# A four-layer graph attention stack: how feature blocks are turned in the third and fourth layer

## The chip, the cores and the metric

The kernel runs on one core of one Trainium2 chip. The metric is the device time of one launch in microseconds (us), from the runs listed below. The engines are named as the profile names them: PE (TensorE, the matrix unit), DVE (VectorE), ACT (ScalarE), POOL (GpSimd) and SP (SyncE). DMAs are issued by an engine, here by SP or POOL, and carried out by 16 DMA engines. Each engine works off its own list of instructions in order; between engines there are semaphores.

## The reference

`x` has 4096 rows (the nodes) of 256 features in float32; `adj` is a 4096 x 4096 matrix of 0 and 1. Four attention layers follow each other, each over all pairs of nodes that `adj` joins, and each ends with a residual sum and a layer norm. The change touches the third and the fourth layer:

```python
# third layer: one additive head
h = x @ W
e = leaky_relu(h @ a[:D, 0] [:, None] + h @ a[D:, 0] [None, :], slope 0.01)
x = layernorm(x + elu(softmax(where(adj > 0, e, -1e12), axis=1) @ h))

# fourth layer: cosine attention
Qn, Kn = cos_normalize(x @ Wq.T), cos_normalize(x @ Wk.T)     # 128 features each
att = softmax(where(adj > 0, Kn @ Qn.T, -9e15), axis=1)
x = layernorm(x + 0.5 * (att @ x) + 0.5 * x)
```

The first layer is additive with four heads, the second is multi-head attention with four heads of 64.

## The kernel before

The features stay in SBUF as `X`, 32 tiles of 128 rows (NT = 32). Four tiles make a block of 512 rows (QB = 4), so there are eight blocks (NB = 8). A projection by PE contracts over features, so it needs a block with the features on the partitions: the block has to be *turned* (transposed) before it. There are two ways to do this in the kernel.

- `transposed_block` (L112): PE transposes eight 128 x 128 pieces into PSUM (L118), and DVE and ACT copy one half each into SBUF (L120). This gives `xT`.
- `turned_apart` (L123), called by `block_apart` (L138) for a block of `X`: DVE transposes 32 x 32 squares within the tiles (two instructions, L130) into a buffer `squares`, one DMA writes it to DRAM (`squares_far`, L133), and four DMAs bring it back, 32 partitions each (L135). The 512 rows of the block come back in another order: the row `k*128 + a*32 + n` of the block stands in tile `a` at place `k*32 + n` (`k` and `a` from 0 to 3, `n` from 0 to 31). A sum over the rows does not depend on their order, so the result is the same if masks, `src`, `dst` and values all keep to it.

**Third layer, `additive_one` (L401).** The loop goes over blocks `b` of columns and, inside, over 32 tiles `j` of rows: 256 units. For each unit ACT forms `e` from the row vector `row` and the scalar `dst` (L451), DVE adds 1 and multiplies by the mask, giving `prob` (L453), and PE adds `prob` times the values `V` into four PSUM accumulators (`sums`, L459, four matmuls). `prob` has three buffers (`gb_z`). A mask tile holds two units, 128 x 2 x 512 int32 or 512 KB, and SP loads it (L449) into one of four buffers. The values `V`, `src` and `dst` of a block come from `project` (L427, matmuls at L196, then ACT at L200 to L202 and DVE at L203). `fill_row` (L431) spreads `src` over all partitions: for block 0 and 1 by PE (L441), for the later ones by two DMAs on POOL's queue, `far<-src` (L436, 512 elements of 4 bytes to DRAM) and `row<-far` (L437, back to 128 partitions).

Blocks 0 and 1 are turned and projected before the loop. Block `n` (2 to 7) is prepared inside `b = 0`: `turn(n)` at `j = 4(n - 2)`, `project(n)` and `fill_row(n)` at `j = 4(n - 2) + 2`. At `j` = 0, 3 and 5 of `b = 0`, the last block of the second layer is finished (`tail`): two sums on POOL (L687), the second of which waits for a DMA, then row sums and turned halves on PE.

**Fourth layer.** Its preparation is class `Cosine`. `prepare(bank, b, step)` (L837) has three steps for each block: step 0 turns the block of `X` (`block_apart`), step 1 projects it (L852), squares and sums it (L857), copies it (L858), takes the roots and multiplies (L863), step 2 turns the result into `T` (`turned_apart`). For blocks 0 to 5 the steps stand in the last block of the third layer (`b = 7`, and step 0 of the first ones at the end of `b = 6`): step 1 of block `n` after unit `2 + 4n`, step 2 after unit `5 + 4n`, step 0 eight units before step 1. Blocks 6 and 7 are prepared in `cosine_attention`, in its first block. All turnings share one `squares` buffer (`co_once`, one buffer). Blocks 0 to 5 issue their DMAs on POOL's queue, blocks 6 and 7 on SP's.

The order of PE's instructions is written by hand in the third layer (`manual_schedule` for PE); for the other engines a scheduler decides it, by what is ready.

Of the kernel before, what the change touches and what calls it, by code (L numbers as in the profile page):

```python
# [9 lines left out]
FP = mybir.dt.float32  # L10
# [8 lines left out]
P = 128  # L19
D = 256  # L20
KC = D // P
QB = 4
QW = QB * P
# [5 lines left out]
def kernel(  # L29
# [27 lines left out]
    nc = tc.nc  # L57
    N = x.shape[0]
    NT = N // P
    NB = N // QW  # L60

    def pool(stack, name, bufs, **kw):
        return stack.enter_context(tc.tile_pool(name=name, bufs=bufs, reuse_waits="tile", **kw))
# [48 lines left out]
    def transposed_block(sb, bank, b, copies=(nc.vector.tensor_copy, nc.scalar.copy)):  # L112

        xT = sb.tile([P, KC * QW], FP, name="xT").rearrange("p (c i) -> p c i", c=KC)
        pts = [bank() for _ in range(KC)]
        for c, pt in enumerate(pts):
            for k in range(QB):
                nc.tensor.transpose(pt[:, k * P:(k + 1) * P], X[:, b * QB + k, c * P:(c + 1) * P], ident)  # L118
        for c, pt in enumerate(pts):
            copies[c](xT[:, c, :], pt)  # L120
        return xT.rearrange("p c (k i) -> p c k i", i=P)

    def turned_apart(once, dr, part, to, eng):  # L123

        B = P // QB
        squares = once.tile([P, QB, KC, P], FP, name="squares")
        for c in range(KC):
            nc.vector.transpose(squares[:, :, c, :].rearrange("p q (k n) -> p k q n", n=B),  # L130
                                part(c).rearrange("p k (q f) -> p k q f", f=B))
        far = dr.tile([QB, B, QB, KC * P], FP, name="squares_far")
        eng.dma_start(far.rearrange("a f q m -> (a f) (q m)"), squares.rearrange("p q c m -> p (q c m)"))  # L133
        for q in range(QB):
            eng.dma_start(to[q * B:(q + 1) * B], far[:, :, q, :].rearrange("a f m -> f a m"))  # L135
        return to.rearrange("p a (c m) -> p c a m", c=KC)
# [264 lines left out]
    def additive_one(w_sb, slope, tail, op, follow):  # L401

        MJ = 2
        mvs, taken = {}, {}
        with ExitStack() as lay:
            keep = pool(lay, "gb_keep", 1)
            V = keep.tile([P, NT, D + 1], FP, name="V")
            src = keep.tile([P, NT, 1], FP, name="src")
            dst = keep.tile([P, NT, 1], FP, name="dst")
            row = keep.tile([P, N], FP, name="row")  # L410
            zp = pool(lay, "gb_z", 3)
            sb = pool(lay, "gb_sb", 2)
            mp = pool(lay, "gb_mask", 4)
            dr = pool(lay, "gb_dram", 2, space=bass.MemoryType.DRAM)

            ps = pool(lay, "gb_ps", 4, space=PSUM)
            pa = pool(lay, "gb_pa", 1, space=PSUM)
            edges = adjT.rearrange("(t p) i -> p t i", p=P)
            mask, acc, prob = {}, {}, {}

# [1 line left out]
                return ps.tile([P, QW], FP, name="g")  # L422

            def turn(b):
                return transposed_block(sb, bank, b)

            def project(b, xT, ks=range(QB)):  # L427
                groups = [(k, 1, bank().rearrange("p (n f) -> p n f", n=1)) for k in ks]
                additive_values(xT, b, groups, w_sb, V, src, dst, 1, slope)

            def fill_row(b):  # L431
                part = row[:, b * QW:(b + 1) * QW]
                if b > 1:

                    far = dr.tile([QB, P], FP, name="far")
                    nc.gpsimd.dma_start(far.rearrange("k p -> p k"), src[:, b * QB:(b + 1) * QB, 0])  # L436
                    nc.gpsimd.dma_start(part, far.rearrange("k p -> (k p)").unsqueeze(0).to_broadcast([P, QW]))  # L437
                    return
                pr = bank()
                for k in range(QB):  # L440
                    nc.tensor.transpose(pr[:, k * P:(k + 1) * P], src[:, b * QB + k, :].to_broadcast([P, P]), ident)  # L441
                nc.scalar.copy(part, pr)

            def weights(b, j):
                cols = slice(b * QW, (b + 1) * QW)
                m = b, j // MJ
                if j % MJ == 0:
                    mask[m] = mp.tile([P, MJ, QW], I32, name="mask")
                    nc.sync.dma_start(mask[m], edges[:, j:j + MJ, cols])  # L449
                e = sb.tile([P, QW], FP, name="e")  # L450
                nc.scalar.activation(e, row[:, cols], AF.Relu, bias=-1.0, scale=dst[:, j, :])  # L451
                prob[b, j] = zp.tile([P, QW], FP, name="prob")
                nc.vector.scalar_tensor_tensor(prob[b, j], e, 1.0, mask[m][:, j % MJ, :], OP.add, OP.mult)  # L453
# [27 lines left out]
            units = [(b, j) for b in range(NB) for j in range(NT)]  # L481
            with tc.manual_schedule(engines={mybir.EngineType.PE}):
                xTs = {0: turn(0), 1: turn(1)}
                project(0, xTs[0])
                project(1, xTs[1], [0, 1])
                fill_row(0)
                project(1, xTs[1], [2, 3])
                for i in range(len(units) + 1):
                    if i < len(units):
                        b, j = units[i]  # L490
                        weights(b, j)

                        if b == 0 and j // QB + 2 < NB:
                            n = j // QB + 2
                            if j % QB == 0:
                                xTs[n] = turn(n)
                            elif j % QB == 2:
                                project(n, xTs[n])
                                fill_row(n)
                    if i:  # L500
                        b, j = units[i - 1]
                        sums(b, j)
                        if (b, j) == (0, 1):
                            fill_row(1)
                        if b == 0 and j in (0, 3, 5):
                            tail(bank, (0, 3, 5).index(j))
                            if j == 5:
                                follow.start()
                        if b and j % 4 == 0 and j // 4 < QB:
                            outputs(b - 1, j // 4)  # L510
                        n, rest = divmod(i - (NB - 1) * NT + 5, 4)
                        if rest == 0 and 0 <= n < NB - 2:
                            follow.prepare(even_bank, n, 0)
                        if b == NB - 1:
                            if j in (6, 10, 14):
                                follow.load_mask(0, (j - 6) // 4, prob[b, j][:, :1])


                            for step, first in enumerate((2, 5), 1):
                                if j >= first and (j - first) % 4 == 0 and (j - first) // 4 < NB - 2:  # L520
                                    follow.prepare(even_bank, (j - first) // 4, step)
                        if j == NT - 1:
                            take_all(b)
# [285 lines left out]
    class Cosine:  # L809

        MJ = 4
# [5 lines left out]
        def start(self):  # L817
            keep = self.stack.enter_context(tc.tile_pool(name="co_keep", bufs=1, side="right", reuse_waits="tile"))
            self.pool = self.stack.enter_context(tc.tile_pool(name="co_in", bufs=2, side="right", reuse_waits="tile"))
            self.masks = self.stack.enter_context(tc.tile_pool(name="co_mask", bufs=4, side="right", reuse_waits="tile"))  # L820
            self.mask = {}

            self.T = [keep.tile([P, QB, 2 * P], FP, name=f"T{b}") for b in range(NB)]
            self.dram = self.stack.enter_context(tc.tile_pool(name="co_dram", bufs=2, space=bass.MemoryType.DRAM))
            self.once = self.stack.enter_context(tc.tile_pool(name="co_once", bufs=1, side="right", reuse_waits="tile"))
            self.w_sb = keep.tile([P, KC, 2 * P], FP, name="w3_sb")
            load_w(self.w_sb[:, :, :P], wq3T, nc.sync)
            load_w(self.w_sb[:, :, P:], wk3T, nc.sync)
# [8 lines left out]
        def prepare(self, bank, b, step):  # L837

            in_, w_sb = self.pool, self.w_sb

            eng = nc.gpsimd if b < NB - 2 else nc.sync
            if step == 0:
                self.xT[b] = block_apart(in_, self.once, self.dram, b, eng)
            elif step == 1:
                xT = self.xT.pop(b)
                norm = in_.tile([P, QB, 2], FP, name="norm")
                rows = self.rows[b] = in_.tile([P, QB, 2, P], FP, name="rows")
                for k in range(0, QB, 2):
                    pr = bank().rearrange("p (t n f) -> p t n f", t=2, f=P)
                    for t in range(2):  # L850
# [12 lines left out]
                nc.vector.tensor_tensor(flat, flat, r.unsqueeze(2).to_broadcast([P, QB * 2, P]), OP.mult)  # L863
            else:
                rows = self.rows.pop(b)
                turned_apart(self.once, self.dram, lambda n: rows[:, :, n, :], self.T[b], eng)

    def cosine_attention(co, tail):
        MJ = co.MJ
        T = [t.rearrange("p k (n i) -> p n k i", n=2) for t in co.T]  # L870
        with ExitStack() as lay:
            sb = pool(lay, "co_sb", 3)
            yp = pool(lay, "co_y", 2)

            pa = pool(lay, "co_pa", 1, space=PSUM)
            pz = pool(lay, "co_pz", 2, space=PSUM)
# [150 lines left out]
```

## Time and profile before

| what | us |
|---|---|
| median of three runs | 2911.56 |
| lowest and highest of them | 2909.53, 2911.84 |
| the profiled execution | 2912.43 |
| its span, first to last instruction | 2910.7 |

The profile is of one execution. A line of its groups names the code line, engine, operation and tile, then how often it ran, its busy time and the mean of one, and what ended the idle time before it. Mean durations of the groups concerned, in the third layer's stretch of the trace:

| group | mean us of one |
|---|---|
| L451, ACT, `e` | 0.721 |
| L453, DVE, `prob` | 0.695 |
| L459, PE, one matmul of 128 x 257 | 0.380 to be busy, 1.735 for the four of a unit and their weights |
| L130, DVE, stream transpose 128 x 512 | 0.69 |
| L120, DVE or ACT copy | 0.68, 0.58 |
| L133, POOL issue of `squares_far<-squares` | 0.56 |
| L135, POOL issue of one of four | 0.555 |
| L436, POOL issue of `far<-src` | 0.776 |

The mean granted clock of PE over the span is 0.997 of full speed.

### The profile page before, as it was taken

The page shows a single profiled execution, that of the slowest core. Times are in us where ns is not written, and L with a number is a line of the kernel's source. Part 1 is how long each engine was busy: PE and PEld are TensorE (multiplying, and loading weights), DVE is VectorE, ACT ScalarE, POOL GpSimd, SP SyncE. Part 2 cuts the span into 40 slices and gives each one's busy share as a digit, 9 for nine tenths or more (in the row PEclk, how much of TensorE's full clock was granted, in tenths as well). Part 3 has the DMA queues.
Part 4 walks back from the last instruction along what each step waited for, and adds up shares of the span by engine and source line. Part 5 has one row for each costly group of instructions (what it writes and reads, how often), then busy time and mean ns, then how long its engine had stood idle before and what let it go on. Part 6 is the DMA issues. An engine that isn't in the chain of part 4 may idle for free.

```text
span 2910.7 us, 50256 instructions
## 1 busy us (share of the span) xinstructions
PE 2889.4 (99%) x20141; PEld 1553.4 (53%) x20141; DVE 1954.2 (67%) x2541; ACT 1655.3 (57%) x2589; POOL 965.2 (33%) x735
## 2 busy tenths in 40 slices
PE   9999999999999999999999999999998999999998
PEld 4333333333643333333333358888887777777776
DVE  8899999998677777777777765655666423333333
ACT  7899999997356666666666654444443222222222
POOL 0010010100068989989889860000012000000000
PEclk9999999999999999999999999999999999999999
DMA  7566667665068989889889875655566434434341
GB/s 205 103 138 137 139 139 145 135 129 90 1 134 193 185 186 193 183 187 192 182 189 191 182 171 133 178 163 150 154 185 168 87 58 58 58 58 58 58 58 29
DMA packets 214061, 391.72 MB, mean 135 GB/s; under 512 B 16338, under 2 KB 94146, under 8 KB 212931
## 3 DMA queue, kind: packets, MB, share of 16 engines
q0 software_dynamic: 106336, 190.35, 40.2%
q1 hardware_dynamic: 107216, 197.88, 22.3%
q8 instruction: 158, 2.59, 0.3%
q14 instruction: 77, 0.62, 0.1%
q10 hardware_dynamic: 274, 0.26, 0.0%
HBM read 325.46 MB, written 29.43 MB: 122 GB/s over the span
## 4 chain that ended last, share of the span: by engine, by line
PE 98%; DMA 1%; DVE 1%; ACT 0%; issue 0%; POOL 0%; DVEq 0%; POOLq 0%
PE acc L293 23%; PE acc L901 15%; PE acc L678 15%; PE p L645 15%; PE acc L459 8%; PE g L459 7%; PE p L889 4%; PE g L889 3%; PE g L572 2%; PE g L196 1%; PE pv L587 1%; PE acc L196 1%; PE g L118 1%; PE acc L852 1%; DMA squares_far<-squares 1%; PE g L305 0%
## 5 line engine op out<-in xcount | busy, mean ns | idle before, releaser
L657 DVE TENSOR_TENSOR prob<-p,mask 128x1024 f32<-128x1024 f32 x512 | 624.1, 1223 | 209.5 <-ACT p L647 203.8
L647 ACT ACTIVATE p<-p,shift 128x1024 f32<-128x1024 f32 x512 | 556.2, 1088 | 325.2 <-PE p L645 324.4
L293 PE MATMUL acc<-prob,V 128*32 128x512 f32 x6144 | 664.0, 592 | 1.2 <-DVE prob L283 1.2
L664 POOL TENSOR_TENSOR den<-den,prob 128x1024 f32<-128x1024 f32 x248 | 626.9, 2528 | 72.6 <-DVE prob L657 64.7
L280 ACT ACTIVATE prob<-row,dst 128x512 f32<-128x512 f32 x1020 | 633.1, 712 | 0.1
L283 DVE SCALAR_TENSOR_TENSOR prob<-prob,mask 128x2048 f32<-128x2048 f32 x256 | 582.5, 2286 | 24.2 <-ACT prob L280 20.7
L645 PE MATMUL p<-qT,kT 64*64 64x512 f32 x4096 | 532.3, 590 | 0.8 <-DVE prob L657 0.8
L678 PE MATMUL acc<-prob,V 64*64 64x512 f32 x4096 | 531.5, 589 | 0.0
L901 PE MATMUL acc<-X,prob 128*128 128x257 f32 x2048 | 485.5, 380 | 0.0
L901 PEld LDWEIGHTS acc<-X,prob 128*128 128x128 f32 x2048 | 388.6, 190 | 162.8 <-issue 112.9
L894 DVE TENSOR_TENSOR prob<-prob,mask 128x512 f32<-128x512 f32 x256 | 176.2, 690 | 409.3 <-ACT prob L893 408.1
L293 PEld LDWEIGHTS acc<-prob,V 128*32 128x32 f32 x6144 | 197.3, 110 | 453.1 <-issue 433.6
L451 ACT ACTIVATE e<-row,dst 128x512 f32<-128x512 f32 x256 | 184.0, 721 | 241.8 <-DVE prob L453 212.6
L678 PEld LDWEIGHTS acc<-prob,V 64*64 64x64 f32 x4096 | 155.9, 133 | 285.4 <-issue 278.1
L645 PEld LDWEIGHTS p<-qT,kT 64*64 64x64 f32 x4096 | 154.4, 133 | 277.3 <-issue 261.5
L453 DVE SCALAR_TENSOR_TENSOR prob<-e,mask 128x512 f32<-128x512 f32 x256 | 177.6, 695 | 173.4 <-PE acc L459 93.9
L91 POOL COPY tick<-prob 128x1 f32<-128x1 f32 x35 | 40.0, 1144 | 645.9 <-DVE prob L283 644.8
L835 POOL DMA_DIRECT2D mask<-in_adjT x64 | 47.6, 743 | 582.2 <-DVE prob L894 505.3
L670 POOL DMA_DIRECT2D den<-prob x240 | 231.6, 965 | 14.7 <-DVE prob L657 7.5
L893 ACT ACTIVATE prob<-p 128x512 f32<-128x512 f32 x144 | 85.7, 596 | 257.0 <-PE p L889 243.0
L459 PE MATMUL acc<-V,prob 128*128 128x257 f32 x1024 | 225.1, 380 | 0.0
L459 PE MATMUL g<-V,prob 128*128 128x257 f32 x1024 | 224.1, 380 | 0.0
(160 smaller groups left out, 1965.6 us busy)
## 6 DMA issues: line engine op xcount, KB each, us to landing
mask<-in_adjT SPq DMA_DIRECT2D x256, 512.0 KB
den<-prob POOLq DMA_DIRECT2D x240, 512.0 KB, 5.3
mask<-edges SPq DMA_DIRECT2D x256, 128.0 KB
mask<-in_adjT POOLq DMA_DIRECT2D x64, 512.0 KB, 5.7
edges<-in_adj POOLq DMA_DIRECT2D x32, 512.0 KB, 10.0
den<-prob SPq DMA_DIRECT2D x16, 512.0 KB
row<-far SPq DMA_DIRECT2D x7, 1024.0 KB
squares_far<-squares POOLq DMA_DIRECT2D x12, 512.0 KB, 4.0
```

Source lines behind the costliest of these rows:

```text
L280: nc.scalar.activation(z[:, h, :], r, AF.Relu, bias=-1.0, scale=dst[:, j, h:h + 1])
L283: nc.vector.scalar_tensor_tensor(z, z, 1.0, mask[m][:, j % MJ, :].unsqueeze(1).to_broadcast([P, H, QW]), OP.add, OP.mult)
L293: nc.tensor.matmul(acc[b][h * G:(h + 1) * G, n, :], part, prob[b, j][:, h, :], start=(j == 0), stop=(j == NT - 1))
L459: nc.tensor.matmul(acc[b][k][:, :D + 1], prob[b, j][:, k * P:(k + 1) * P], V[:, j, :], start=(j == 0), stop=(j == NT - 1))
L645: nc.tensor.matmul(p[c * d:(c + 1) * d, r, :], kT[half, c, j * d:(j + 1) * d], qT[half, c, cols], start=True, stop=True)
L647: nc.scalar.activation(p, p, AF.Exp, bias=shift)
L657: nc.vector.tensor_tensor(z, p, mask[m][:, j % MJ, :].unsqueeze(1).to_broadcast([P, KC, QW]), OP.mult)
L664: nc.gpsimd.tensor_tensor(to, to, flat, OP.add)
L670: nc.gpsimd.dma_start(to, flat, accum_op=OP.add)
L678: nc.tensor.matmul(acc[b][c][r * d:(r + 1) * d, :], V[half, j, r * d:(r + 1) * d], prob[b, j][half, r, :], start=(j == 0), stop=(j == NH - 1))
L889: nc.tensor.matmul(p.rearrange("p (k i) -> p k i", k=QB), T[j // QB][:, 0, j % QB], T[b][:, 1], start=True, stop=True)
L901: nc.tensor.matmul(acc[b][k], prob[b, j][:, k * P:(k + 1) * P], X[:, j, :], start=(j == 0), stop=(j == NT - 1))
```

## The change

Three things are changed. Line numbers here are those of the kernel before.

1. Third layer: blocks 2 to 7 are turned by `block_apart` (DVE and POOL's queue) and not by PE. Block 2 is turned before the loop, block `n + 1` at `j = 4(n - 2)`, one group of four units ahead of its projection. The turning gets pools of its own: three `xT` buffers, one `squares` buffer, two DRAM buffers.
2. The rows of these blocks stand in the other order. Masks of rows from the ninth tile on are fetched by four DMAs of 32 partitions each, in the order of the turned block, and `far<-src` becomes four DMAs of 32 x 4 elements.
3. Fourth layer: step 0 is issued on SP's queue and uses the third layer's turning pools (later a set of the same in the fourth layer). Step 2 stays on POOL's queue (SP for blocks 6 and 7), with a squares buffer of its own. The tile `rows` comes from `co_once`, with one buffer and not two.

```diff
-    def turned_apart(once, dr, part, to, eng):
+    def turned_apart(squares, far, part, to, eng):
         B = P // QB
-        squares = once.tile([P, QB, KC, P], FP, name="squares")
+        squares = squares.tile([P, QB, KC, P], FP, name="squares")
+        far = far.tile([QB, B, QB, KC * P], FP, name="far")
...
+            xp = pool(lay, "gb_turn", 3)
+            sq = pool(lay, "gb_squares", 1)
+            far = pool(lay, "gb_far", 2, space=bass.MemoryType.DRAM)
+            follow.turning = xp, sq, far
...
+            apart = adjT.rearrange("(b k a n) i -> k n b a i", k=QB, a=QB, n=P // QB)
...
             def turn(b):
-                return transposed_block(sb, bank, b)
+                return transposed_block(xp, bank, b)
+            def turn_apart(b):
+                return block_apart(*follow.turning, b, nc.gpsimd)
...
-                    far = dr.tile([QB, P], FP, name="far")
-                    nc.gpsimd.dma_start(far.rearrange("k p -> p k"), src[:, b * QB:(b + 1) * QB, 0])
-                    nc.gpsimd.dma_start(part, far.rearrange("k p -> (k p)").unsqueeze(0).to_broadcast([P, QW]))
+                    far = dr.tile([QB, QB, P // QB], FP, name="far")
+                    for k in range(QB):
+                        at = slice(k * P // QB, (k + 1) * P // QB)
+                        nc.gpsimd.dma_start(far[k].rearrange("a n -> n a"), src[at, b * QB:(b + 1) * QB, 0])
+                    nc.gpsimd.dma_start(part, far.rearrange("k a n -> (k a n)").unsqueeze(0).to_broadcast([P, QW]))
...
                     mask[m] = mp.tile([P, MJ, QW], I32, name="mask")
-                    nc.sync.dma_start(mask[m], edges[:, j:j + MJ, cols])
+                    if j < 2 * QB:
+                        nc.sync.dma_start(mask[m], edges[:, j:j + MJ, cols])
+                    else:
+                        for k in range(QB):
+                            nc.sync.dma_start(mask[m][k * P // QB:(k + 1) * P // QB],
+                                              apart[k, :, j // QB, j % QB:j % QB + MJ, cols])
...
                 xTs = {0: turn(0), 1: turn(1)}
+                xTs[2] = turn_apart(2)
                 project(0, xTs[0])
...
                             n = j // QB + 2
-                            if j % QB == 0:
-                                xTs[n] = turn(n)
+                            if j % QB == 0 and n + 1 < NB:
+                                xTs[n + 1] = turn_apart(n + 1)
                             elif j % QB == 2:
                                 project(n, xTs[n])
                                 fill_row(n)
...
-            self.dram = self.stack.enter_context(tc.tile_pool(name="co_dram", bufs=2, space=bass.MemoryType.DRAM))
             self.once = self.stack.enter_context(tc.tile_pool(name="co_once", bufs=1, side="right", reuse_waits="tile"))
+            self.far = self.stack.enter_context(tc.tile_pool(name="co_far", bufs=2, space=bass.MemoryType.DRAM))
...
-            eng = nc.gpsimd if b < NB - 2 else nc.sync
             if step == 0:
-                self.xT[b] = block_apart(in_, self.once, self.dram, b, eng)
+                self.xT[b] = block_apart(*self.turning, b, nc.sync)
             elif step == 1:
...
-                rows = self.rows[b] = in_.tile([P, QB, 2, P], FP, name="rows")
+                rows = self.rows[b] = self.once.tile([P, QB, 2, P], FP, name="rows")
...
-                turned_apart(self.once, self.dram, lambda n: rows[:, :, n, :], self.T[b], eng)
+                turned_apart(self.once, self.far, lambda n: rows[:, :, n, :], self.T[b],
+                             nc.gpsimd if b < NB - 2 else nc.sync)
...
+            co.turning = (pool(lay, "co_turn", 2), pool(lay, "co_squares", 1),
+                          pool(lay, "co_turn_far", 2, space=bass.MemoryType.DRAM))
```

More of the change, by code (lines that the diff above doesn't have):

```diff
@@ L131, in turned_apart @@
                                 part(c).rearrange("p k (q f) -> p k q f", f=B))
-        far = dr.tile([QB, B, QB, KC * P], FP, name="squares_far")
         eng.dma_start(far.rearrange("a f q m -> (a f) (q m)"), squares.rearrange("p q c m -> p (q c m)"))
```

## The prediction

> **What bounds the kernel now.** I read the page's busy table and the shares of the chain first, then TensorE's waits, then the chain piece by piece through the third layer, then POOL and DVE in time at the two places that the change touches.
>
> ```profile
> PE 2889.4 (99%) x20141; PEld 1553.4 (53%) x20141; DVE 1954.2 (67%) x2541; ACT 1655.3 (57%) x2589; POOL 965.2 (33%) x735
> ...
> PE 98%; DMA 1%; DVE 1%; ACT 0%; issue 0%; POOL 0%; DVEq 0%; POOLq 0%
> ```
>
> TensorE is the bound everywhere: 2889.4 of 2910.7 us. A change gains only TensorE work that goes, or TensorE idle time that goes, and any new wait of TensorE is paid in full. The waits:
>
> ```profile
> PE acc L852 <- DMA xT<-squares_far: 8.7, 2, 7.9
> PE acc L293 <- DVE prob L283: 1.2, 1, 1.2
> ```
>
> One wait stands out, of 7.9 us, in the fourth layer's preparation. The chain there:
>
> ```profile
> 2170.09 3.47 PE acc L852 x16
> ...
> 2175.23 7.20 DMA squares_far<-squares
> ...
> 2185.20 8.59 DMA squares_far<-squares
> ...
> 2195.96 3.61 DMA xT<-squares_far
> 2199.57 0.24 issue
> 2199.81 6.55 PE acc L852 x16
> ```
>
> Two preparations share one squares buffer and one queue: the T squares of one block must land before the next block's squares can be turned, and L852 of group 3 starts 7.9 us late. It then takes 6.55 us, not 3.47: over 2195.6 to 2205.9 the granted clock is 0.51, after 2191.9 to 2199.8 with TensorE idle. So the stall costs 0.8 + 7.9 + 3.1 (second wait, first wait, slow matmuls) + 0.2 (issue) = 12.0 us.
>
> The turning in the third layer, from the same chain in block 0:
>
> ```profile
> 1757.61 3.47 PE acc L459 x16
> 1761.08 0.87 PE g L118 x8
> 1761.95 3.47 PE acc L459 x16
> 1765.42 3.49 PE g L196 x16
> ```
>
> Four units take 2 x 3.47 + 0.87 + 3.49 = 11.30 us; a turn by TensorE is 0.87 of it, with no wait around it.
>
> POOL at the start of the third layer:
>
> ```profile
> 1718.53 2.36 POOL L687 TENSOR_TENSOR den<-den 128x1024 f32<-128x1024 f32 x1 [1.76 <-DMA den<-prob]
> 1720.83 0.87 POOL L670 DMA_DIRECT2D den<-prob  x1
> 1727.75 2.34 POOL L687 TENSOR_TENSOR den<-den 128x1024 f32<-128x1024 f32 x1 [6.04 <-DMA den<-prob]
> 1734.32 0.84 POOL L436 DMA_DIRECT2D far<-src  x1 [4.23 <-ACT V L202]
> 1743.15 0.56 POOL L437 DMA_DIRECT2D row<-far  x1 [8.00 <-DMA far<-src]
> 1745.50 0.77 POOL L436 DMA_DIRECT2D far<-src  x1 [1.79 <-ACT V L202]
> 1757.06 0.54 POOL L437 DMA_DIRECT2D row<-far  x1 [10.79 <-DMA far<-src]
> ```
>
> Until 1730.1 POOL is held by the second layer's joining of sums, which waits 6.04 us for its own DMA; and each L437 stands 8 to 10.8 us at the head of POOL's queue, waiting for L436's small DMA.
>
> **What the skill says.** "TensorE: Matmul & The Clock Gate", Part 1: after an idle window of about 3.4 us the array runs at half clock until a busy window has passed. The trace agrees (0.51, L852 at 6.55 us). The same page, in the detail on queue depths: ACT and DVE are strict FIFO, so what stands behind a waiting instruction waits too; POOL's L437 shows it here. "DMA: Bandwidth & Descriptors", Specifications: transfers under 512 B are a read-modify-write; here far<-src, 512 elements of 4 B, takes 10.8 us to land (median) where the 512 KB of squares_far take 4.0. The same page, Issuing engines are not separate DMA queues: a second issuing queue saves issue time and no bandwidth. What two queues can save here is the 0.55 us an issue and the standing behind another's wait, no more.
>
> **The change part by part.** I take it against the profiled execution, 2912.43 us (span 2910.7), 0.9 above the median 2911.56. Order is what the built kernels' instruction lists show engine by engine.
>
> *B, six turns off TensorE.* 6 x 0.87 = 5.2 us; block 2's is used up inside A, so 5 x 0.87 = -4.35. DVE takes two stream transposes (0.69 each) in place of one PSUM copy (0.68), ACT loses one of 0.59; in block 0 DVE is busy 6.7 of 11.3 us, so that is hidden.
>
> *A, block 2 at the start of the layer.* On POOL the DMA squares to DRAM of block 2 comes after both joins: issued about 1730.3. It lands 4.0 to 4.6 us later, say 1734.7. On DVE the squares of block 3 (one squares buffer, so they wait for that landing) stand ahead of the prob of unit (0,0). 1734.7 + 2 x 0.69 + one V product (0.42) + 0.69 gives prob at about 1737.3. Before, the sums of unit (0,0) started at 1727.24. The four xT DMAs of block 2 issue from 1734.7 (2.2 us) and land about 1740.5. The projection of block 2 starts there instead of at 1728.98: it ends at about 1744.5 where it ended at 1732.47. That is +12.0 (its own turn of 0.87 already taken off). TensorE has been idle over 10 us, so its clock falls; the earlier case of this cost 3.1. I add 3 (bounds 0 and 4, as the sums at 1737.3 may warm it).
>
> *C, POOL's queue in block 0.* Per group POOL now issues four far<-src (4 x 0.77 at most), the squares of the next block, row<-far (waits far<-src), then four xT (2.2). The far<-src wait heads the queue as before, and the next block's xT lies behind it. If four far<-src side by side land like the one, POOL's cycle is 10.8 + 2.75 = 13.55 us, against TensorE's new 10.43. From the end of block 2's projection to the start of block 7's are 5 x 10.43 - 3.49 = 48.7 us; the last xT takes some 3.9 of it to be issued and land (xT lands 3.7 after issue), which leaves 44.8. POOL needs the first landing (8.0 by the first L437's wait above, 10.8 at the median) and three cycles: 48.7 to 51.5 with 13.55, a stall of 3.9 to 6.7. At 10.6 a cycle (quarters landing sooner) it is 0; at 16.8, each quarter landing as late as a whole one after its own later issue, 18.7. I take +3, as quarters should land a little sooner than wholes, and keep 0 and 18.7.
>
> *Quarter masks.* 96 of 128 masks become four DMAs: 4 x 0.37 = 1.5 us of SP issue per 3.47 us of two units; the bytes are the same, in rows of 2 KB as before (packets of 2 KB take 0.084 us each on 16 engines at 0.52 to 0.66 share). Four buffers give about 14 us of lead. Nothing; if it failed, each mask late by x costs x, and I keep 0 to 5. The SP steps of the fourth layer stand among these issues but SP has room.
>
> *D, the preparation.* Step 0 goes to SP with three turned buffers: xT of each block is there over 10 us before L852. The stall of 12.0 and its slow matmuls go. What is late next is DVE. Before, DVE worked off probs between the pieces of a step:
>
> ```profile
> 2173.03 0.69 DVE L858 COPY rows<-acc 128x512 f32<-128x512 f32 x1 [1.36 <-ACT sq L857]
> 2174.86 0.65 DVE L858 COPY rows<-acc 128x512 f32<-128x512 f32 x1
> 2175.50 0.68 DVE L453 SCALAR_TENSOR_TENSOR prob<-e,mask 128x512 f32<-128x512 f32 x1
> 2176.91 1.22 DVE L863 TENSOR_TENSOR rows<-rows,r 128x1024 f32<-128x1024 f32 x1
> 2178.06 1.48 DVE L453 SCALAR_TENSOR_TENSOR prob<-e,mask 128x512 f32<-128x512 f32 x2
> ```
>
> The T squares came later, behind probs. In the changed order, for groups 1, 2 and 3 both copies, the root, the product L863 and the two T squares all stand ahead of the prob of the next unit. From L852's start (2170.09) the product ends 8.04 us later (2178.13); plus 1.29 of squares and 0.69 of prob makes 10.0. TensorE has L852 and one unit of sums meanwhile, 3.45 + 1.74 = 5.19: a stall of about 4.9 for groups 2 and 3. For group 1 a layer norm and a squares turning stand ahead too, 7.0. Groups 0, 4, 5 by the same count: 2.4, 1.9, 0.9. Sum 22.1. Each idle piece is longer than the window in three cases, so half-clock pieces follow: 1 to 1.5 each, +4 (0 to 8). D is 22.1 + 4 - 12.0 = +14.1.
>
> Sum: 12.0 + 3 - 4.35 + 3 + 14.1 = +27.8, so 2940.2 for a profiled run and 2939 on the median.
>
> **Rivals.**
> - *POOL's queue decides.* C at its upper end, 18.7 in place of 3: 2955. For it: L437's waits of 8.00 and 10.79 head the queue, and the landing of four DMAs at once isn't in the trace. Against it: each has a quarter of the elements.
> - *The preparation's order costs nothing* (the other side: not slower). If DVE gets through group n's chain in 5.2 us, or TensorE is fed from the three prob buffers so that prob of the next unit isn't needed by then, D is -12.0 and the sum 12 + 3 - 4.35 + 3 - 12 = +1.7: 2913. It decides when prob of unit 8 is ready within 5.2 us of L852's start. For it: before, DVE never held TensorE in that stretch with the same work. Against: then three probs had run ahead, and in the new order only one has.
> - *The change does what it is written to.* No stall at the start, none in the preparation: -5.2 - 12.0 = -17.2: 2894. It needs the squares of block 2 on their way before 1724, but POOL has a wait of 6.04 us in front of them.
> - *Masks by quarters become the bound*: were each of the 96 masks 0.5 us late, +48: 2987. SP's 1.5 of 3.47 us and the unchanged bytes speak against it; that issuing on SP isn't seen four deep in the trace speaks for it.
>
> **How the numbers follow.** Forecast 0.60 (own range 2922 to 2952: cold pieces at 0 and DVE stalls at 15 below, C at 10 and cold pieces at 8 above). POOL's queue 0.15, masks 0.03. The preparation free 0.12. All gained 0.10. A measurement of this kernel tells 0.2% (5.8 us) from no change. Faster is the last case and a little of the one before: 0.12. Same, 2905.7 to 2917.4, is most of the free preparation: 0.12. Slower 0.76. The range reaches from the free preparation to POOL's queue with some cold pieces: 2911 to 2959; the masks' case and the full gain are left out.
>
> **What would show it.** A: TensorE idle between about 1726 and 1740, the sums of unit (0,0) waiting for DVE, L196 of block 2 for the DMA of xT, and DVE's block 3 squares waiting some 10 us for a DMA. B: 48 fewer L118. C: row<-far waits on POOL growing, L196 waiting for xT in later groups. D: no wait of L852 for the DMA of xT, but sums waiting for DVE's prob about 5 us three times, granted clock at 0.5 beside. If TensorE shows no DVE wait in block 7, D is wrong; if the first projection isn't late, A is.

## The result

| kernel | median us | lowest to highest | runs | ratio to before, 95% interval |
|---|---|---|---|---|
| before | 2911.7 | 2909.53 to 2913.19 | 4 | 1 |
| changed | 2951.01 | 2946.63 to 2953.6 | 4 | 1.0134 [1.0119, 1.0149] |

The change costs 39 us. Line numbers below are those of each kernel's own code: in the changed one L459 has become L476, L453 L470, L451 L468, L130 L131, L852 L868, L858 L874, L863 L879, L441 L452, L436 and L437 L447 and L448, and the masks' L449 L461 and L465. The profiled execution of the changed kernel took 2952.2 us (span 2950.4), 39.8 over the one of before. First its busy table and the shares of its chain:

```profile
PE 2895.4 (98%) x20093; PEld 1554.7 (53%) x20093; DVE 1956.0 (66%) x2547; ACT 1652.9 (56%) x2583; POOL 974.5 (33%) x753
...
PE 94%; DMA 3%; DVE 2%; POOL 1%; ACT 1%; issue 0%; SPq 0%; DVEq 0%; POOLq 0%; ACTq 0%
```

There are 48 matmuls fewer, and yet TensorE is busy 6 us longer (2889.4 before): some pieces run at half clock (the granted clock is 0.50 over 1734.9 to 1738.3 us, for one). The chain now leaves TensorE for 6% of the span. TensorE's waits (line, what it waited for, sum, times, longest):

```profile
PE g L476 <- DVE prob L470: 18.7, 5, 6.4
PE acc L476 <- DVE prob L470: 15.4, 3, 9.0
PE g L196 <- DMA xT<-far: 5.9, 1, 5.9
PE g L196 <- ACT e L468: 1.7, 1, 1.7
```

The old wait of L852 (now L868) for xT is gone. Waits for `prob` have come in two places, `acc` in the third layer's first block and `g` in its last, and one for a turned block. At the start of the third layer the chain leads to the first of them as follows (start, duration, what):

```profile
1720.40 6.76 DMA den<-prob
...
1727.31 2.29 POOL den L705
1729.59 2.96 DMA far<-squares
...
1732.65 0.06 DVE squares L131
...
1734.29 0.58 DVE prob L470
...
1734.91 3.79 PE acc L476 x8
```

POOL's second sum waits for its DMA, the squares of block 2 go out behind it, and DVE, whose next instruction turns block 3 into the one squares buffer, stands until they have landed; the first `prob` stands behind that. TensorE in time in the first block, from the changed kernel's timeline (start, duration, wait before in brackets):

```profile
1734.91 3.79 PE L476 MATMUL acc<-V,prob 128*128 128x257 f32 x8 [9.02 <-DVE prob L470]
1738.50 4.86 PE L196 MATMUL g<-w_sb,xT 128*128 128x258 f32 x16
...
1791.44 3.80 PE L476 MATMUL acc<-V,prob 128*128 128x257 f32 x8 [4.85 <-DVE prob L470]
...
1811.69 5.81 PE L196 MATMUL g<-w_sb,xT 128*128 128x258 f32 x16 [5.86 <-DMA xT<-far]
```

Eight matmuls of L476 take 1.9 us in this view at full clock ("warm"), a projection 3.65. After each of these waits, of 4.85 to 9.02 us, the first piece takes about 2 us longer; after the 9.02 us the projection behind it takes 1.2 us longer as well. The last projection ends at 1817.50, where it ended at 1791.52 before; the first one, of block 2, at 1743.36 (1732.47). The layer itself began 0.5 us earlier in this execution. So the start of the layer costs 11.4 us, and the following five groups 15.1 although five turns are gone.

The last block, same view:

```profile
2190.17 1.90 PE L476 MATMUL g<-V,prob 128*128 128x257 f32 x8
2198.50 7.00 PE L476 MATMUL g<-V,prob 128*128 128x257 f32 x24 [6.43 <-DVE prob L470]
2205.34 3.62 PE L868 MATMUL acc<-w_sb,xT 128*128 128x256 f32 x16
2208.79 1.90 PE L476 MATMUL g<-V,prob 128*128 128x257 f32 x8
2215.51 7.03 PE L476 MATMUL g<-V,prob 128*128 128x257 f32 x24 [4.82 <-DVE prob L470]
```

After each step's L868 there is one unit of sums, then the wait. 24 matmuls take 5.37 us warm in this view, here 7.0. DVE in the first of these waits, from its timeline:

```profile
2190.61 0.65 DVE L874 COPY rows<-acc 128x512 f32<-128x512 f32 x1
...
2191.80 0.65 DVE L874 COPY rows<-acc 128x512 f32<-128x512 f32 x1
...
2193.85 1.23 DVE L879 TENSOR_TENSOR rows<-rows,r 128x1024 f32<-128x1024 f32 x1
2196.57 1.30 DVE L131 STREAM_TRANSPOSE squares<-rows 128x512 f32<-128x512 f32 x2 [1.49 <-DMA far<-squares]
2197.79 1.25 DVE L470 SCALAR_TENSOR_TENSOR prob<-e,mask 128x512 f32<-128x512 f32 x2
```

No `prob` stands between the copies, the product and the squares of the step. 1.49 us of this wait is one for the landing of the squares before, which hold the buffer.

From the first L868 to that of block 6 the preparation is 115.1 us long, where it was 99.9: +15.2. Of this 1.7 us is no delay: six matmuls of the fourth layer (two of `p`, four of `acc`) that stood behind block 6's projection before stand ahead of it now. The delay is 13.4 us.

POOL in the same execution, one cycle of its queue:

```profile
1775.13 2.17 POOL L447 DMA_DIRECT2D far<-src  x4
1777.29 0.56 POOL L133 DMA_DIRECT2D far<-squares  x1
1788.49 0.56 POOL L448 DMA_DIRECT2D row<-far  x1 [10.64 <-DMA far<-squares]
1789.38 2.21 POOL L135 DMA_DIRECT2D xT<-far  x4 [0.34 <-issue]
1791.58 2.17 POOL L447 DMA_DIRECT2D far<-src  x4
```

It takes 16.5 us from one set of far<-src to the next. `row<-far` waits for its far<-src by the code; the view puts the wait down to far<-squares, which landed at about the same time. The next xT stands behind it.

### The profile page after: what moved, and what is told of

Its sections match the earlier page's. It is cut to its first block, busy times and chain, and to the rows that moved or that the text cites. A ratio compares the mean times of both kernels' runs of the same rounds, so it can differ in the third digit from the quotient of the medians.

```text
span 2950.4 us, 50714 instructions
## 1 busy us (share of the span) xinstructions
PE 2895.4 (98%) x20093; PEld 1554.7 (53%) x20093; DVE 1956.0 (66%) x2547; ACT 1652.9 (56%) x2583; POOL 974.5 (33%) x753
## 4 chain that ended last, share of the span: by engine, by line
PE 94%; DMA 3%; DVE 2%; POOL 1%; ACT 1%; issue 0%; SPq 0%; DVEq 0%; POOLq 0%; ACTq 0%
PE acc L293 22%; PE acc L921 15%; PE p L663 15%; PE acc L696 15%; PE g L476 7%; PE acc L476 7%; PE p L909 4%; PE g L909 3%; PE g L590 2%; DMA far<-squares 2%; PE pv L605 1%; PE g L196 1%; PE acc L196 1%; DMA den<-prob 1%; PE acc L868 0%
## 5 line engine op out<-in xcount | busy, mean ns | idle before, releaser
L468 ACT ACTIVATE e<-row,dst 128x512 f32<-128x512 f32 x256 | 183.3, 721 | 273.5 <-DVE prob L470 245.3
L470 DVE SCALAR_TENSOR_TENSOR prob<-e,mask 128x512 f32<-128x512 f32 x256 | 175.1, 687 | 172.8 <-PE acc L476 89.0
L476 PE MATMUL g<-V,prob 128*128 128x257 f32 x1024 | 230.2, 386 | 18.8 <-DVE prob L470 18.7
L476 PE MATMUL acc<-V,prob 128*128 128x257 f32 x1024 | 228.5, 384 | 15.4 <-DVE prob L470 15.4
```

Of the source, the lines that this page charges most:

```text
L476: nc.tensor.matmul(acc[b][k][:, :D + 1], prob[b, j][:, k * P:(k + 1) * P], V[:, j, :], start=(j == 0), stop=(j == NT - 1))
```

## The experiments

Three losses had to be told apart: A, at the start of the third layer; C, in the rest of its first block; D, in the fourth layer's preparation. The first four kernels test each in turn.

**1. Step 0 on POOL's queue.** It tests whether D is DVE's order.

```diff
-                self.xT[b] = block_apart(*self.turning, b, nc.sync)
+                self.xT[b] = block_apart(*self.turning, b, nc.gpsimd if b < NB - 2 else nc.sync)
```

> Changed kernel, but step 0 of blocks 0 to 5 is issued on POOL's queue and not on SP's (its buffers stay separate). In the built order of DVE this brings back one or two prob instructions between the pieces of each preparation step; nothing of the third layer's block 0 changes. Theory (DVE's order makes the preparation's stalls, two separate buffers remove the old one): from 2951 the stalls for prob in the preparation (19.5 us) and their half-clock pieces go, the old stall of 12 does not come back: 2920 to 2928. Rival (prob is late there because the quartered masks are late, or because DVE has too much work): the stalls stay and it is 2946 to 2954. Second rival (the queue itself was the old bottleneck): the old wait of L868 for xT comes back, 2935 or more.

2927.53 us (2925.51 to 2930.45), ratio 1.0055 [1.0038, 1.0072]: within what the theory gave. All of TensorE's waits for `prob` in the last block are gone. In DVE's timeline of this kernel a `prob` stands again between the copies and the product of a step (in the second step at 2187.87 us) and between the product and the squares (2190.43). The chain there, start, duration, what:

```profile
2172.07 3.45 PE acc L868 x16
2175.53 6.94 PE g L476 x32
2182.47 3.45 PE acc L868 x16
```

The masks are still quartered, DVE's work is the same, and both turnings of a block go through POOL's queue again without the old wait: the old stall was the shared squares buffer with what hung on it, not the queue alone.

**2. The preparation's change alone**, with the third layer as before.

> Changed kernel's fourth-layer preparation (two queues, separate buffers) with the third layer as before: PE turns, whole masks, one far<-src. Theory: without the quartered masks DVE's built order keeps probs between the pieces, so only the old stall of 12.0 goes: 2897 to 2902, faster than the kernel before. Rival (two queues only shift the bound to DVE): stalls for prob as in the changed kernel, 2920 to 2928.

2900.15 us (2899.23 to 2900.61), ratio 0.9957 [0.9942, 0.9972]: faster than before by 12. From the first step's matmuls to those of block 6 it takes 87.7 us, 12.2 less than before (predicted for the stall: 12.0). Two queues are harmless while the masks are whole. So D needs both: quartered masks on SP and step 0 on SP. With both, DVE's order has no `prob` between the copies, the product and the squares of a step; in experiments 1 and 2, with one of the two undone, it has.

**3. All third-layer turning on SP's queue.**

```diff
-                return block_apart(*follow.turning, b, nc.gpsimd)
+                return block_apart(*follow.turning, b, nc.sync)
```

> Changed kernel, but the third layer's turned blocks 2 to 7 are moved by DMAs on SP's queue and not POOL's. Same bytes and same pieces. Theory (POOL's queue: the joining sums before it at the start, and the wait for far<-src at its head later): the 26 us lost up to the last projection go and the turns' 5 are gained; the preparation's 15 stay: 2917 to 2925. Rival (DMA traffic makes the landings late, whichever queue issues): the waits of L196 for xT and of prob behind the squares stay, 2940 to 2950.

2944.32 us (2942.5 to 2944.95), ratio 1.0108 [1.0093, 1.0123]. The theory fails here, and the time lies among the rival's numbers. The start did improve: block 2's projection starts at 1731.44, not 1738.50. Later it is lost again, for two reasons that the trace shows: transfers land late, and the masks stand behind xT. SP's queue, from that kernel's timeline:

```profile
1727.31 0.44 SPq L133 DMA_DIRECT2D far<-squares  x1
1728.22 1.18 SPq L465 DMA_DIRECT2D mask<-in_adjT  x2
1732.73 1.73 SPq L135 DMA_DIRECT2D xT<-far  x4
...
1761.04 0.35 SPq L133 DMA_DIRECT2D far<-squares  x1
1761.66 1.02 SPq L465 DMA_DIRECT2D mask<-in_adjT  x2
1773.03 2.54 SPq L135 DMA_DIRECT2D xT<-far  x4
```

The squares issued at 1727.31, with no far<-src under way, let xT go 5.4 us later. Those issued at 1761.04, just after POOL's far<-src of 1759.32, hold it for 12.0. And while xT waits for its squares at the head of SP's queue, the masks behind it aren't issued. DVE's waits for masks:

```profile
1763.01 1.29 DVE L470 SCALAR_TENSOR_TENSOR prob<-e,mask 128x512 f32<-128x512 f32 x2 [3.38 <-DMA mask<-in_adjT]
1770.82 1.29 DVE L470 SCALAR_TENSOR_TENSOR prob<-e,mask 128x512 f32<-128x512 f32 x2 [6.51 <-DMA mask<-in_adjT]
...
1795.71 1.29 DVE L470 SCALAR_TENSOR_TENSOR prob<-e,mask 128x512 f32<-128x512 f32 x2 [4.34 <-DMA mask<-in_adjT]
```

The 6.51 us are for a mask whose last quarter SP issued at 1760.19, ahead of the xT of 1773.03: that mask landed late, beside far<-src and the squares. The 4.34 us are for one whose last two quarters stood behind the next xT, which SP held from 1780.8 to 1787.47.

The Trainium skill says in "DMA: Bandwidth & Descriptors", Issuing engines are not separate DMA queues, that DMAs issued by different engines run on the same 16 DMA engines and interleave, so that another issuing engine saves only issue time. This run agrees: squares issued on SP are late (12.0 us) while POOL's far<-src is under way.

**4. Only block 2 on SP's queue.**

> Changed kernel, but only block 2's DMAs are on SP's queue; blocks 3 to 7 stay on POOL's. Theory: only the stall at the start of the layer goes (11 to 14 us), the cycle of POOL's queue that is longer than TensorE's group stays: 2936 to 2942. Rival (the two are one: with the start early the later groups only wait longer, since POOL's cycle sets when the last xT lands): gain of 0 to 6 only, 2945 to 2951.

2945.49 us (2943.4 to 2947.94), ratio 1.0114 [1.0099, 1.0129]: the rival's numbers. Block 2's projection starts at 1731.45, 7 us earlier, but waits of 7.5 and 7.9 us for `prob` follow in the next groups, and the whole gains 5.5. A and C can't be added up as if they were apart: of the 8.1 us that A costs less in the profiled execution, C takes back 2.6.

The theory for C was revised after this: the small elements of far<-src slow what is in flight with them, whichever queue issues it, and hold the head of POOL's queue besides. The next four kernels test it.

**5. Rows filled by PE.** far<-src and row<-far are gone; ACT's copy puts the columns in order.

```diff
-                if b > 1:
-                    far = dr.tile([QB, QB, P // QB], FP, name="far")
...
-                nc.scalar.copy(part, pr)
+                if b > 1:
+                    nc.scalar.copy(part.rearrange("p (k a n) -> p k a n", k=QB, a=QB),
+                                   pr.rearrange("p (a k n) -> p k a n", k=QB, a=QB))
+                else:
+                    nc.scalar.copy(part, pr)
```

> Changed kernel, but fill_row of blocks 2 to 7 is done by PE and an ACT copy that puts the columns into their order (6 x 0.44 us more of PE), so that far<-src and row<-far are gone; the turning stays on POOL's queue. Theory (the wait for far<-src at the head of POOL's queue makes the cycle): POOL's cycle shrinks to squares and xT, the last projection starts near 1800 and not 1811.7, total 2937 to 2943. Rival (the DMA engines, which carry masks and turned blocks together, make each landing late): squares still land 8 to 11 us after their issue, gain of 0 to 4 less 2.6 for PE, 2948 to 2954.

2937.77 us (2935.95 to 2938.24), ratio 1.0087 [1.0072, 1.0102]: within the theory's numbers. TensorE's only wait in that block is the one at the start:

```profile
PE acc L471 <- DVE prob L465: 10.6, 1, 10.6
```

The DMA view of 1735 to 1815 us, first the changed kernel, then this one (the last number is the median time to landing in us):

```profile
xT<-far POOLq DMA_DIRECT2D x22, 128.0 KB, 4.5
far<-squares POOLq DMA_DIRECT2D x5, 512.0 KB, 8.7
```

```profile
xT<-far POOLq DMA_DIRECT2D x24, 128.0 KB, 3.0
far<-squares POOLq DMA_DIRECT2D x5, 512.0 KB, 4.9
```

Without the small elements (2 KB a block) and the rows that follow them, 512 KB land 3.8 us sooner. A group of four units then takes 11.02 us with nothing waited for: 0.59 of it is the row by PE, and the rest, 10.43, is the old group less one turn of 0.87. From the end of the first projection to that of the last it takes 57.6 us, 1.4 less than before the change, as five turns less and five rows more come to. So C is gone, while A stands. Whether the late landings or the wait at the head of POOL's queue weighed more is not told apart here, as both went.

**6. Two squares buffers in the third layer.**

```diff
-            sq = pool(lay, "gb_squares", 1)
+            sq = pool(lay, "gb_squares", 2)
```

> Changed kernel with two squares buffers in the third layer. Theory (DVE waits for a landing before it may turn the next block, and prob stands behind): TensorE's waits for prob in block 0 (15.4 us) go, among them the 9.0 at the start; L196's waits for xT grow, because the queue is as before, so that about half is given back: 2940 to 2947. Rival (the single buffer decides all): 2930 to 2936. Second rival (the queue decides all): no change, 2948 to 2953.

2947.34 us (2943.09 to 2949.2), ratio 1.0119 [1.0104, 1.0134]. It is at most 4 us better, just past the theory's upper edge, and the expectation that the waits for `prob` go was half wrong:

```profile
PE acc L476 <- DVE prob L470: 10.1, 1, 10.1
PE g L196 <- DMA xT<-far: 4.1, 1, 4.1
```

The two later waits for `prob` (4.85 and 1.53 us) went, the one at the start did not: with a second buffer the scheduler moves yet another block's squares ahead of the first `prob`, and those wait in turn.

**7. Turned by PE, quartered masks and four far<-src kept.** The copies out of PSUM put the rows into the new order.

> Changed kernel, but blocks 2 to 7 are turned by PE and the copies put the rows into the new order; the quartered masks, the four far<-src and step 0 on SP's queue stay. Theory (the turning's DMAs and squares make the third layer's loss; quartered masks cost nothing by themselves but lead to DVE's order in the preparation): block 0 of the third layer as before the change, the last projection near 1788, stalls for prob in the preparation as in the changed kernel: 2924 to 2930. Rival (the quartered masks or the four far<-src carry the third layer's loss): 2940 or more.

2926.88 us (2926.38 to 2929.31), ratio 1.0052 [1.0038, 1.0067]. TensorE waits for nothing between 1700 and 1850 us, and far<-src in four parts lands in 8.1 us. So quartered masks and split far<-src by themselves cost the third layer nothing; the turning's DMAs beside them do. In the last block it has waits for `prob` as the changed kernel has, 21.4 us of them; of the longest, 8.97, DVE spends 4.03 waiting for squares to land.

**8. The first eight masks used again in block 0**, so that 12 masks of 512 KB fewer are fetched there.

> Changed kernel, but in block 0 of the third layer the units from the ninth on use the masks of the first eight again: 12 masks of 512 KB less are fetched while the blocks are turned, and the sums of that block's columns are other ones. Everything else is in place. Theory (order on POOL's queue and the landing time of small elements): the stalls shrink by a third at most, 2942 to 2950. Rival (contention of the DMA engines with the masks): landings fall to 4 to 6 us and most of the 19 us goes, 2930 to 2937.

2942.16 us (2940.43 to 2944.15), ratio 1.0101 [1.0084, 1.0118]. It is at the near edge of the theory's numbers and outside the rival's. `row<-far` waits 6.8 to 7.3 us in place of 6.8 to 10.6, and squares still take 8.5 us to land. Here a row<-far is issued only 7 to 8 us after the squares (1759.52 and 1767.33 in one group), and no mask is fetched: what is under way with them is far<-src. But the stalls shrink by more than the third that the theory allowed: from the end of the first projection to that of the last it takes 63.4 us, 10.8 less than in the changed kernel (74.1). The preparation is 2.9 us longer in this execution, which hides a part of it in the total. So in these two executions the masks under way make about half of C's 19.4 us, and the rival was half right. In experiment 5 masks are fetched and C is gone: the loss needs the small elements (or the rows behind them, which went with them), and the masks beside them about double it.

**9. `prob` ahead of each chain**, the queues as in the changed kernel. The weights of one more unit are emitted before a step, and the step's copies (and likewise its first operation for the root) are ordered behind it.

```diff
+                        if b == NB - 1 and j % 4 == 2 and j < 26:
+                            early.add(i + 1)
+                            weights(b, j + 2)
...
-                    nc.vector.tensor_copy(rows[:, k:k + 2], pr)
+                    with tc.issue_after(self.last) if b < NB - 2 else nullcontext():
+                        nc.vector.tensor_copy(rows[:, k:k + 2], pr)
```

> Changed kernel with nothing but DVE's and ACT's order changed in the last block of the third layer: prob of two more units is put ahead of each preparation step's chain (queues, pieces, and the orders of PE and SP are the changed kernel's). Theory (the stalls of the preparation are DVE's order alone): with 8.65 us of PE's work in hand and the next prob at about 10.7 us from L868's start, each of the three stalls of 4.8 to 6.4 falls to about 2, and the half-clock pieces of 1.8 behind them go: 2934 to 2941. Rival (late masks, or step 0 on SP's queue): the stalls stay, 2947 to 2953.

2944.79 us (2939.78 to 2946.01), ratio 1.0112 [1.0095, 1.0128]. The profiled run, 2939.78, the fastest of the four, lies among the theory's numbers; the median lies above them and below the rival's. In the profiled run the waits fell as counted, from 18.7 us to

```profile
PE g L477 <- DVE prob L470: 8.5, 6, 1.9
```

with none above 1.9, and the preparation took 102.8 us in place of 115.1. A new wait came up where the order allowed it, DVE's for a mask, 4.30 us once: SP's step 0 stands before it. So order alone, of DVE and of ACT, which forms the `e` of the unit brought forward, gives back 12.3 us. Against experiment 2's preparation with the six matmuls added, 89.4, the changed kernel lost 25.7, so this is about half. Late masks, my rival here, are the next thing under it; how the other half divides is not shown, nor is what the other three runs of this kernel, 4 to 6 us slower, waited for.

**10. All three taken away.** Block 2 by PE as before; blocks 3 to 7 by DVE and POOL, two squares buffers, each turning ordered behind its own unit's `prob`; rows by PE; step 0 on POOL.

> The three causes taken away together: block 2 turned by PE as before the change, blocks 3 to 7 turned by DVE and POOL's DMAs with two squares buffers and each turning put behind the prob of its own unit; rows of blocks 2 to 7 filled by PE (no far<-src); step 0 of the preparation on POOL's queue. Theory, counted from the kernel with only the preparation changed (2900): five turns less (-4.35), six rows by PE more (+2.64), and the 3.8 us by which the first experiment's preparation was longer than that kernel's: 2898 to 2905. Rival (a further cost of the turning, by contention of the DMA engines or of DVE, which the experiments so far did not part from the three): 2910 or more.

2899.86 us (2899.66 to 2900.77), ratio 0.9957 [0.9942, 0.9971]. Within the theory's numbers, and TensorE has no wait over 0.4 us in either place. The preparation was 0.9 us longer than that of experiment 2, not 3.8 (of those 3.8, 1.7 was the six matmuls named above). This is the changed kernel's idea without its waits, and it is no better than experiment 2 at 2900.15, which leaves the third layer alone: five turns gained against six rows paid.

## Why the prediction was right, and where it was off

It forecast 2939 with a range of 2911 to 2959 and the slower side; 2951 came out. The direction was right, and so was the mechanism of A and of D. In C it was right only in part, and there the size was far off. By its steps, in the profiled executions:

| step | predicted us | measured us |
|---|---|---|
| A, start of the layer, with slow clock | +15.0 | +11.4 |
| B, five turns | -4.35 | -4.35 (counted; experiment 5's groups agree) |
| C, POOL's queue in block 0 | +3, bounds 0 and 18.7 | +19.4 (15.1 and the 4.35 of B) |
| D, preparation | +14.1 | +13.4 |

They come to 39.9, and rounding, the layer's start and the rest of the fourth layer make up the difference to 39.8. Of the 12 us by which the forecast was too low, C is 16.4; A and D, both put too high, take 3.6 and 0.7 back, which is luck.

- *A was right.* `prob` was predicted for 1737.3, the projection's end for 1744.5 before slow clock; it was 1734.9 and 1743.36. The squares landed in 3.0 us and not in 4.0 to 4.6; the 175 GB/s that moved then are these 512 KB alone. The slow clock cost 1.9 + 1.2 us, the 3 taken. DVE's squares waiting for the landing (9.03 us by DVE's timeline), with `prob` behind, was the mechanism, as the chain above has it. One sign did not come: the projection of block 2 had no wait for xT, as the slow sums before it lasted until 1738.5. A fix of A alone gave only 5.5 (experiment 4), as C grew in return.
- *B stands.* L118 is down by 48, and a group of experiment 5 without its row takes 10.43 us, the 11.30 of before less 0.87.
- *C was mis-sized, at +3 for 19.4.* The step took the four quarters of far<-src as landing "a little sooner than wholes", for a POOL cycle of at most 13.55 us. The cycles were 13.5, 17.8, 16.5 and 14.3, mean 15.5. The waits of row<-far, which were to grow, did not: the longest was 10.6 us, 11.3 before. Three things were left out. Squares beside far<-src land late (8.7 us, 4.9 without). DVE stands still with the squares buffer, so that `prob` is late inside the groups too: of TensorE's 14.1 us of waits there, only 5.9 are the predicted wait for xT, 6.4 are for `prob` (1.5 and 4.9), 1.7 for `e`. And each wait drags slow matmuls behind it, 4.3 us in all. The measured 19.4 lies just outside the upper bound of 18.7; in experiment 1's execution, whose third layer has the same code, it is 17.4. By time the rival "POOL's queue decides", at 2955 and a chance of 0.15, was nearer than the forecast.
- *Quartered masks were costed at nothing and cost nothing in themselves in the third layer* (experiment 7). Their indirect price is D: with them and step 0 on SP, and only with both, the scheduler gave DVE another order (experiments 1 and 2). The four far<-src are not needed for it: experiment 5, without them, has 17.7 us of these waits.
- *D was right, with two errors that cancel in part.* The waits were predicted as 7.0, 4.9, 4.9 and 5.2 in the others, 22.1 (these parts add up to 22.0); they were 6.43, 4.82, 4.82 and 3.4, in sum 19.5, the last 0.7 of it a wait for ACT at the fourth layer's start. The slow clock was put at +4; it was 3 x 1.65 = 5. The old stall was 12.0 by the prediction, 12.2 by experiment 2. These make 12.3 of the 13.4; what the other 1.1 is, is not shown. In the first wait 1.49 us went to a landing that the count did not have. The waits rest on an order of instructions that could be read before the run.
- *The rival "preparation's order costs nothing"* fell where the order was as built, and came true once the order was another (experiment 1). The full gain, 2894, was not reached by any kernel; 2899.86 came nearest to it with the third layer changed.

## What to carry to other kernels

Moving a step to a second queue can change the order that a scheduler gives an engine which the move doesn't touch: read the built order of the engine that feeds the bound one before pricing the move, since 12 us of gain became 13 us of loss here, about half of that way by order alone (experiment 9). A wait at the head of a shared queue can't be priced from its landing time in a quieter stretch when the change itself puts 512 KB beside it. Before replacing 0.87 us of the busiest engine with DMAs, ask what else in the block uses small elements; taking these away, with the rows that follow them, was worth more here (13.2 us, experiment 5) than all six turns (5.2).

## What the runs showed of the hardware

- Small elements slowed large transfers here: 512 KB of squares landed in 4.9 us (median) with no far<-src in the block and in 8.7 beside it, on the same queue (and in 8.5 with no masks fetched). In the changed kernel the squares issued before any far<-src landed in 3.0 us, and later ones, each just behind one, in 8.5 to 11.5. With the squares on SP and far<-src on POOL, xT had to wait 12.0 us for squares beside a far<-src and 5.4 for squares without.
- A wait of TensorE of 4.8 us cost 1.65 us more in slow matmuls after it (7.03 for 24 in place of 5.37), so about a third on top; one of 9.0 us cost about 3.1 us more, in eight matmuls and a projection.
- The first block's waits vary between executions: the last projection started at 1811.69 in the changed kernel, with 1811.86 in the kernel of experiment 9, which has the same order there, but experiment 1's run, also of that order, had 5.6 us of waits for xT in three pieces and not in one.
